# Twelve steps of seven tiles instead of fourteen of six, in a graph layer on one Trainium2 core

## The chip, the core and the metric

The kernel runs on one core of a Trainium2 chip. Its engines have queues of their own: PE multiplies matrices (PEld loads their weights), ACT and DVE work on whole tiles, POOL issues the gathers, and SP issues the direct loads and stores. The metric is the device time of one execution in microseconds; three runs of the kernel before were taken, and one further execution was profiled.

## The reference

The inputs are 6250 nodes with 64 features each, and 206250 edges that are sorted by their destination. The layer adds up, for each node, the normed features of its neighbours and the features of its edges, and puts the sum through two dense layers:

```python
h = jnp.maximum(_layernorm(x, axis=-1), 0.0)
msg = h[src] + edge_attr_64
agg = jax.ops.segment_sum(msg, dst, num_segments=6250)
x = x + (jax.nn.relu(agg @ W1 + b1) @ W2 + b2)
```

## The kernel before

**Neighbours by counting.** The sum over neighbours is a product of a matrix of counts (how often node `s` is a source for destination `d`) with `h`. The counts are made tile by tile. A tile holds up to 127 edges of three neighbouring destinations; 84 tiles are a block of 252 destinations, and 23 blocks make up the whole. For a tile DVE makes a row of one-hot digits (`encode`, L943 and L949, then `rows_of_tiles`, L960, into `hotb`), PE multiplies them (`count`, L973, one weight load and one product of 49 columns per tile, into `pc`, which has two buffers), and ACT copies the counts from `pc` into `ring` (L983). 49 products per block (`products`, L996) then multiply `ring` with `h`, each for 128 sources and all 252 columns of the block, into `pv`; a row of `ring` is one of these 49. The products of block b run while the counts of block b+1 are made.

**Steps.** The program is written step by step, and each engine takes its instructions in the order in which the steps were written. A step stands for `ST` = 6 tiles, a block has 14 steps, and each odd step counts a pair of steps, 12 tiles, and copies them in one instruction of 128 x 1764 elements. The last pair of a block is copied in two pieces: first the rows 0 to 12 of the 49 (432 elements), which the first run of products needs, then the other 37 (1332 elements). `PART` divides the 49 products in runs of 12, 12, 12 and 13, at the steps 1, 3, 5 and 7 of the next block. `ring` has a block's 252 columns and 144 fresh ones (`FRESH` = 8 steps), into which odd blocks write their first steps.

**Edge features.** Each block has six chunks of edges. SP loads them (`feat`), DVE makes their one-hot matrix (`hotf`, L505), PE sums them by node (`chunk_sum`, L518, into `bank`) at the steps 9, 11 and 11 of a block, and `chunk_place` (L550) adds the sums to `pv` at step 3. The last 17 groups of edges go another way: POOL gathers neighbour rows onto them (L361), PE sums them (L581), ACT copies (L583), DVE adds (L563).

**The order of the rest** is a set of tables by step number: which step turns the digits of 128 tiles (`TURNS`), clears `sums` (`CLEARS`), splits `h` into an upper and a lower part by thirds (`UPPERS`, ACT, L635; `LOWERS`, DVE, L639), or runs the second layer of a finished block (`LAYERS`; L1074, L1076, L1082, L1088).

**The head.** Before the steps come the layer norm and the first searches for where each tile's edges begin (`seek`, L384, on ACT). Five late searches stand behind the steps 5 to 9, and `place` (L389, L391, DVE) takes them up at step 10. Then a chain of small steps finds the tiles (up to fourteen) whose destinations have more than 127 edges: `second_ends` (L829, L830 on DVE; `pnext`, L832 on PE), `second_flags` (L839), `second_ranks` (L845, L847), `second_picks` (L861), `second_words` (L869). The first edge chunks wait for their destinations: a gather (`dstq`), `chunk_nodes` (L456, L457, DVE, step 5), and `chunk_turn` at step 6 (`pdst`, L464 on PE, and the copy into `rel`, L465 on ACT), which `hotf` reads.

## Time and profile before

| | us |
|---|---|
| median of three runs | 396.44 |
| lowest and highest of the three | 394.69, 398.32 |
| the profiled execution | 398.41 |
| span of the profile, first to last instruction | 396.7 |

The profiled execution lies 1.97 us above the median of the runs. The granted TensorE clock is 0.998 of full speed. In a list by engines the busy times overlap, since the engines work side by side; a busy share says nothing of who waits. The chain of waits is a path backwards from the last instruction; its shares add up to the span.

### The profile page before, as it was taken

Reading aid. Unit: us, or ns where it says so; the run is one execution under the profiler, and the core shown is the slowest. Engines: PE = TensorE matmul, PEld = TensorE weight load, DVE = VectorE, ACT = ScalarE, POOL = GpSimd, SP = SyncE. Lnnn points to the kernel's source line nnn. Section 1 sums busy time; section 2 is a strip of 40 time slices with the busy share of each in tenths; the row PEclk is TensorE's granted clock in tenths of the full one; section 3 lists DMA queues with packets and bytes.
Section 4 is the critical chain, followed back from the end, with each engine's and each line's share of the span. In section 5 each row is a group of like instructions: output and inputs, shape, how many; then the busy total and the mean of one; then the engine's idle time right before and its main releaser. Section 6 shows DMA issues by size and latency. Waiting matters only on the chain.

```text
span 396.7 us, 17221 instructions
## 1 busy us (share of the span) xinstructions
PE 339.1 (85%) x7303; PEld 308.0 (78%) x7304; DVE 307.0 (77%) x804; ACT 326.7 (82%) x380; POOL 268.0 (68%) x204
## 2 busy tenths in 40 slices
PE   2063589889989999999999799999999999999993
PEld 1052278779878879988899799989889889988983
DVE  5989477989986877968887788968886978696641
ACT  7586858798989779988799899988899889987750
POOL 7737768857857786668867578676866776766500
PEclk9999999999999999999999999999999999999999
DMA  8969765969865958869769669867958967887600
GB/s 170 266 202 327 238 172 99 256 158 226 216 181 130 266 131 215 238 142 267 190 167 258 180 158 266 235 160 206 257 127 220 269 176 181 212 215 176 165 10 25
DMA packets 111947, 76.89 MB, mean 194 GB/s; under 512 B 30855, under 2 KB 107775, under 8 KB 111865
## 3 DMA queue, kind: packets, MB, share of 16 engines
q1 hardware_dynamic: 91134, 67.20, 56.9%
q0 software_dynamic: 20560, 8.28, 15.9%
q8 instruction: 59, 0.97, 1.0%
q10 hardware_dynamic: 171, 0.26, 0.2%
q14 instruction: 23, 0.19, 0.2%
HBM read 71.45 MB, written 4.26 MB: 191 GB/s over the span
## 4 chain that ended last, share of the span: by engine, by line
PE 71%; ACT 12%; issue 7%; DVE 5%; DMA 3%; POOL 0%; DVEq 0%; ACTq 0%; SPq 0%; POOLq 0%
PE pv L996 30%; PE bank L518 14%; PE pc L973 12%; ACT ring L983 8%; PE ph L1074 3%; PE pv L550 2%; PE po L1082 2%; PE bank L581 2%; DMA dstq<-in_dst_g,cols_i 2%; PE pk L772 2%; DMA xl<-in_x 1%; ACT kq L792 1%; DVE sums L602 1%; ACT over L908 1%; PE pdst L464 1%
## 5 line engine op out<-in xcount | busy, mean ns | idle before, releaser
L983 ACT ACTIVATE ring<-pc 128x1764 fp32r<-128x1764 uint8 (+3 forms) x184 | 262.1, 1476 | 31.8 <-PE pc L973 19.3
L361 POOL DMA_INDIRECT pfeat<-table,src_p x132 | 222.3, 1684 | 80.0 <-PE bank L518 47.7
L996 PE MATMUL pv<-ring,h 128*128 128x252 f32 x1127 | 155.7, 287 | 10.6 <-ACT ring L983 6.0
L996 PEld LDWEIGHTS pv<-ring,h 128*128 128x128 f32 x1127 | 138.2, 190 | 13.2 <-ACT ring L983 7.2
L960 DVE TENSOR_TENSOR hotb<-at,of 127x576 int32<-127x576 bf16 x216 | 120.2, 599 | 2.1 <-PE pc L973 0.8
L973 PE MATMUL pc<-hotb 128*128 128x49 fp8e5 x1932 | 77.8, 186 | 4.4 <-ACT ring L983 2.3
L973 PEld LDWEIGHTS <-hotb 128*128 128x128 fp8e5 x1932 | 67.9, 98 | 14.1 <-issue 3.8
L518 PE MATMUL bank<-feat,hotf 128*18 128x64 f32 x3288 | 67.2, 224 | 7.7 <-issue 7.0
L518 PEld LDWEIGHTS bank<-feat,hotf 128*18 128x18 f32 x3288 | 52.6, 99 | 16.0 <-issue 13.3
L505 DVE TENSOR_TENSOR hotf<-rel,iota 128x432 f32<-128x432 bf16 x69 | 41.5, 601 | 6.3 <-PE ph L1074 3.0
L1031 DVE TENSOR_TENSOR sums<-sums,pv 128x252 f32<-128x252 f32 (+2 forms) x27 | 8.1, 328 | 23.8 <-PE pv L996 20.6
L943 DVE TENSOR_TENSOR at<-iota_a,kq 128x576 bf16<-128x576 bf16 (+1 forms) x54 | 24.2, 449 | 0.4
L307 PE MATMUL psrc<-shift,src 128*64 128x128 f32 (+1 forms) x16 | 4.1, 433 | 18.8 <-ACT src L304 18.8
L361 POOL DMA_INDIRECT words<-packed,first_i x15 | 16.4, 1091 | 5.6 <-issue 4.3
L361 POOL DMA_INDIRECT sums<-in_dst_g,row_i x15 | 16.2, 1079 | 4.8 <-issue 4.0
L949 DVE TENSOR_TENSOR of<-of,kv 128x288 bf16<-128x288 bf16 (+1 forms) x54 | 16.6, 308 | 2.6 <-ACT kv L800 0.2
L792 ACT ACTIVATE kq<-pk 128x512 bf16<-128x512 f32 (+18 forms) x48 | 17.9, 456 | 0.3 <-PE pc L973 0.3
L307 PEld LDWEIGHTS psrc<-shift,src 128*64 128x64 f32 (+1 forms) x16 | 3.1, 243 | 18.8 <-ACT src L304 14.1
L1074 PE MATMUL ph<-sums,w1s 128*128 128x252 f32 (+2 forms) x48 | 16.1, 416 | 1.9 <-ACT over L908 1.6
L943 DVE TENSOR_TENSOR of<-iota_w,kq 128x288 bf16<-128x288 bf16 (+1 forms) x54 | 16.2, 301 | 0.9 <-ACT kq L792 0.9
L1076 ACT ACTIVATE after<-ph,b1s 128x252 f32<-128x252 f32 (+2 forms) x24 | 11.5, 480 | 4.7 <-PE ph L1074 3.3
L1082 PE MATMUL po<-w2s,after 128*126 128x64 f32 (+2 forms) x96 | 15.1, 280 | 0.0
(190 smaller groups left out, 301.6 us busy)
## 6 DMA issues: line engine op xcount, KB each, us to landing
feat<-in_edge SPq DMA_DIRECT2D x137, 384.0 KB
pfeat<-in_edge SPq DMA_DIRECT2D x16, 256.0 KB
pfeat<-table,src_p POOLq DMA_INDIRECT x132
xl<-in_x SPq DMA_DIRECT2D x3, 512.0 KB
out_y<-after SPq DMA_DIRECT2D x22, 63.0 KB
table<-xl SPq DMA_DIRECT2D x2, 512.0 KB
after<-in_x SPq DMA_DIRECT2D x4, 252.0 KB
table<-xl SPq DMA_DIRECT2D x1, 544.0 KB
```

What stands on the lines that cost most here:

```text
L361: ins = nc.gpsimd.indirect_dma_start(out=rows, out_offset=None, in_=source, in_offset=bass.IndirectOffsetOnAxis(ap=index, axis=0), compute ...
L505: nc.vector.tensor_tensor(hot_of[u][:, :n].rearrange("p c j w -> p (c j) w"), rel[:, c:c + n].rearrange("p c q k -> p (c q k)").unsqueeze( ...
L518: ins = nc.tensor.matmul(bank[q * QP:q * QP + WQ, at:at + D], hot_of[u][:, c, j, :], feats[u][c][:, j, :], start=(k == 0), stop=(k == JP - 1))
L792: nc.scalar.activation(kq[:, q, at:at + n].rearrange("s i k o -> s (i k) o"), pk[:, q, a:a + n].rearrange("s i k -> s (i k)").unsqueeze(2) ...
L943: nc.vector.tensor_tensor(to[:, :n].rearrange("s i k (m o) -> s (i k) m o", o=2), iota_k.rearrange("s (m o) -> s m o", o=2).unsqueeze(1).t ...
L949: nc.vector.tensor_tensor(pairs_of, pairs_of, kv[:, c:c + n].rearrange("s i k o -> s (i k) o").unsqueeze(2) .to_broadcast([P, 2 * n, WE // ...
L960: nc.vector.tensor_tensor(hot[:SLOTS, :n, c:c + m * A8].rearrange("s i (w a) -> s i w a", a=A8), at[:SLOTS, o:o + n, k].unsqueeze(2).to_br ...
L973: nc.tensor.matmul(pc[:, j * WPC:j * WPC + HI], hot[:, :P], hot[:, P:P + HI], start=True, stop=True)
L983: done.append(nc.scalar.activation(to[:, h:z, :mid - u], of[:, h:z, u:mid, :V], AF.Copy))
L996: nc.tensor.matmul(pvs[b], h2[:, h, :], ring[:, h, c:c + columns_of_block(b)], start=(h == 0), stop=(h == HI - 1))
L1074: nc.tensor.matmul(ph[:, :n], w1s, agg[:, start[b]:start[b + 1]], start=True, stop=True)
L1082: nc.tensor.matmul(po[:pairs[b], k, :], hid[:, k:2 * pairs[b]:2], w2s, start=True, stop=True)
```

## The change

A step stands for seven tiles instead of six, and a block has twelve steps instead of fourteen. A pair is 14 tiles, so that a block has six counts and six copies (the last still in two pieces) instead of seven. The block's products run in three runs of 16, 16 and 17, at the steps 1, 3 and 5, and the first piece of the last copy holds 16 of the 49 rows. `ring` has 126 fresh columns (`FRESH` = 6 steps of 21 columns). `encode` takes 42 tiles at once instead of 36, `rows_of_tiles` 21 instead of 18. All tables by step number are scaled to the new steps, some by a step more or less. In the head the first `chunk_turn` moves from step 6 to step 5, ahead of the first late search.

```diff
-ST = 6
+ST = 7
-FRESH = 8
+FRESH = 6
-LOWERS = (11, 15, 17)
+LOWERS = (10, 13, 15)
-FIRST = 12
-PART = (0, 0, 12, 12, 24, 24, 36, 36, HI)
+FIRST = 16
+PART = (0, 0, 16, 16, 32, 32, HI)
-CHUNKS = ((9, 9), (11, 11), (11, 11))
+CHUNKS = ((7, 7), (9, 9), (9, 9))
-FIRST_CHUNKS = ((9, 9), (11, 11), (15, 15))
+FIRST_CHUNKS = ((8, 8), (10, 10), (13, 13))
...
-LAYERS = {10: 3, 5: 2}
+LAYERS = {8: 3, 4: 2}
...
-EB = 36
-HT = 18
-R = 7 * EB
+EB = 42
+HT = 21
+R = 6 * EB
...
     before = {
         2: [lambda: [fetch_h(g) for g in range(GA, GA + ROWS)]],
-        5: [lambda: chunk_nodes(0)],
-        6: [lambda: chunk_turn(0)],
+        4: [lambda: chunk_nodes(0)],
+        5: [lambda: chunk_turn(0)],
         10: [lambda: place(7, 8)],
```

How the order moves is shown at three places. In each row stands the line, the operation, what is written and what is read, and the size; numbers behind a name tell buffers apart, and the waits are by engine or DMA queue.

The first place is ACT in the head, from the third copy of counts (before) to the last late search:

```order
L983 ACTIVATE ring_402<-pc_486 128x49x36 [waits PE_49]
L384 ACTIVATE sums_72,first_215<-sums_72,nhalf_207 128x256 [waits DMASW5_49,Activation_49]
L635 ACTIVATE h2_73<-xl_93 128x16x64
L465 ACTIVATE rel_217<-pdst_503 128x384 [waits PE_49]
L384 ACTIVATE sums_72,first_215<-sums_72,nhalf_207 128x256 [waits DMASW6_49,Activation_49]
L983 ACTIVATE ring_402<-pc_512 128x49x36 [waits PE_49]
L384 ACTIVATE sums_72,first_215<-sums_72,nhalf_207 128x256 [waits DMASW7_49,Activation_49]
L635 ACTIVATE h2_73<-xl_93 128x16x64 [waits DVE_49]
L384 ACTIVATE sums_72,first_215<-sums_72,nhalf_207 128x256 [waits DMASW0_49,Activation_49]
L983 ACTIVATE ring_402<-pc_538 128x49x36 [waits PE_49]
L384 ACTIVATE sums_72,first_215<-sums_72,nhalf_207 128x256 [waits DMASW1_49,Activation_49]
```

The same place in the changed kernel, from the first split of `h`, which stands behind the second copy:

```order
L635 ACTIVATE h2_73<-xl_93 128x16x64
L465 ACTIVATE rel_217<-pdst_491 128x384 [waits PE_49]
L983 ACTIVATE ring_402<-pc_496 128x49x42 [waits PE_49]
L384 ACTIVATE sums_72,first_215<-sums_72,nhalf_207 128x256 [waits DMASW5_49,Activation_49]
L635 ACTIVATE h2_73<-xl_93 128x16x64 [waits DVE_49]
L384 ACTIVATE sums_72,first_215<-sums_72,nhalf_207 128x256 [waits DMASW6_49,Activation_49]
L983 ACTIVATE ring_402<-pc_521 128x49x42 [waits PE_49]
L384 ACTIVATE sums_72,first_215<-sums_72,nhalf_207 128x256 [waits DMASW7_49,Activation_49]
L635 ACTIVATE h2_73<-xl_93 128x17x64 [waits DVE_49]
L384 ACTIVATE sums_72,first_215<-sums_72,nhalf_207 128x256 [waits DMASW0_49,Activation_49]
L983 ACTIVATE ring_402<-pc_582 128x49x42 [waits PE_49]
L384 ACTIVATE sums_72,first_215<-sums_72,nhalf_207 128x256 [waits DMASW1_49,Activation_49]
```

The copy into `rel` (L465) has moved ahead of the third copy and of the first late search; three copies of counts now stand between it and the last search, where two stood.

The second place is DVE in the head, at the `place` that takes up the late searches (128x8). Before:

```order
L389 SCALAR_TENSOR_TENSOR first_215<-first_215,middle_205 128x8 [waits Activation_49]
L391 TENSOR_TENSOR first_i_216<-first_215,limit_212 128x8 [waits DVE_49]
L829 MEMSET ends_593 128x1
L830 TENSOR_SCALAR ends_593<-first_215 128x15
L639 TENSOR_TENSOR h2_73<-xl_93,h2_73 128x16x64
L839 SCALAR_TENSOR_TENSOR flag_601<-pnext_596,ends_593 128x15 [waits DVE_49,PE_49]
```

In the changed kernel:

```order
L389 SCALAR_TENSOR_TENSOR first_215<-first_215,middle_205 128x8 [waits Activation_49]
L391 TENSOR_TENSOR first_i_216<-first_215,limit_212 128x8 [waits DVE_49]
L639 TENSOR_TENSOR h2_73<-xl_93,h2_73 128x16x64
L829 MEMSET ends_638 128x1
L830 TENSOR_SCALAR ends_638<-first_215 128x15
L839 SCALAR_TENSOR_TENSOR flag_644<-pnext_641,ends_638 128x15 [waits DVE_49,PE_49]
```

The lower part of the first third of `h` (L639) now stands between `place` and `ends`, which `pnext` on PE reads.

The third place is ACT in a late block (no digits are turned there), from the first piece of a block's last copy to the last whole copy of the next. Before:

```order
L983 ACTIVATE ring_402<-pc_7359 128x12x36 [waits PE_49,Activation_49]
L983 ACTIVATE ring_402<-pc_7359 128x37x36 [waits Activation_49]
L983 ACTIVATE ring_402<-pc_7382 128x49x36 [waits PE_49]
L983 ACTIVATE ring_402<-pc_7417 128x49x36 [waits PE_49]
L583 ACTIVATE after_280<-bank_199 128x42 [waits DVE_49,PE_49]
L983 ACTIVATE ring_402<-pc_7465 128x49x36 [waits PE_49]
L983 ACTIVATE ring_402<-pc_7496 128x49x36 [waits PE_49]
L983 ACTIVATE ring_402<-pc_7529 128x49x36 [waits PE_49,Activation_49]
L1076 ACTIVATE after_280<-ph_7581,b1s_257 128x252 [waits PE_49,Activation_49]
L983 ACTIVATE ring_402<-pc_7584 128x49x36 [waits PE_49,Activation_49]
```

In the changed kernel:

```order
L983 ACTIVATE ring_402<-pc_7242 128x16x42 [waits PE_49,Activation_49]
L983 ACTIVATE ring_402<-pc_7242 128x33x42 [waits Activation_49]
L983 ACTIVATE ring_402<-pc_7267 128x49x42 [waits PE_49]
L983 ACTIVATE ring_402<-pc_7308 128x49x42 [waits PE_49]
L583 ACTIVATE after_280<-bank_199 128x42 [waits DVE_49,PE_49]
L983 ACTIVATE ring_402<-pc_7362 128x49x42 [waits PE_49]
L983 ACTIVATE ring_402<-pc_7401 128x49x42 [waits PE_49,Activation_49]
L1076 ACTIVATE after_280<-ph_7458,b1s_257 128x252 [waits PE_49,Activation_49]
L983 ACTIVATE ring_402<-pc_7461 128x49x42 [waits PE_49,Activation_49]
```

One whole copy is gone, each of the others is a sixth longer, and the first piece has 16 rows of 42 instead of 12 rows of 36.

## Rows read from the trace of the kernel before

**Rows 1.** Page, parts 1 and 4: busy time; chain by engine and line
```profile
PE 339.1 (85%) x7303; PEld 308.0 (78%) x7304; DVE 307.0 (77%) x804; ACT 326.7 (82%) x380; POOL 268.0 (68%) x204
...
PE 71%; ACT 12%; issue 7%; DVE 5%; DMA 3%; POOL 0%; DVEq 0%; ACTq 0%; SPq 0%; POOLq 0%
PE pv L996 30%; PE bank L518 14%; PE pc L973 12%; ACT ring L983 8%; PE ph L1074 3%; PE pv L550 2%; PE po L1082 2%; PE bank L581 2%; DMA dstq<-in_dst_g,cols_i 2%; PE pk L772 2%; DMA xl<-in_x 1%; ACT kq L792 1%; DVE sums L602 1%; ACT over L908 1%; PE pdst L464 1%
```

**Rows 2.** Windows: stretch, length, busy (x) of PE, PEld, DVE, ACT, POOL
```profile
0.00:56.58 56.58, 23.10 (x311) 17.55 (x312) 40.40 (x108) 38.48 (x69) 38.15 (x63) 1.00 0.85 239
56.58:253.69 197.11, 184.34 (x4108) 169.05 (x4109) 164.60 (x435) 174.02 (x196) 144.09 (x90) 1.00 0.76 194
253.69:367.20 113.51, 108.16 (x2491) 99.90 (x2491) 90.06 (x223) 100.67 (x102) 80.87 (x51) 1.00 0.79 205
367.20:396.70 29.50, 23.46 (x396) 21.46 (x396) 11.96 (x41) 13.52 (x16) 4.93 (x3) 0.98 0.25 65
```

**Rows 3.** Groups by shape, ACT copies: busy us, mean ns, idle before
```profile
L983 ACT ACTIVATE ring<-pc 128x1764 fp32r<-128x1764 uint8 x137 | 223.6, 1673 | 11.0 <-PE pc L973 7.5 <-PE pv L996 1.2 <-PE pnext L833 1.2
...
L983 ACT ACTIVATE ring<-pc 128x1332 fp32r<-128x1332 uint8 x22 | 28.2, 1280 | 0.0
...
L983 ACT ACTIVATE ring<-pc 128x432 fp32r<-128x432 uint8 x22 | 11.7, 531 | 20.8 <-PE pc L973 11.8 <-PE pk L772 9.0
```

**Rows 4.** Timeline of PE, block 15: start us, us, instruction [idle before]
```profile
266.08 0.47 PE L973 MATMUL pc<-hotb 128*128 128x49 fp8e5 x12
...
266.88 0.46 PE L973 MATMUL pc<-hotb 128*128 128x49 fp8e5 x12
268.16 1.67 PE L996 MATMUL pv<-ring,h 128*128 128x252 f32 x12 [0.82 <-ACT ring L983]
269.68 0.47 PE L973 MATMUL pc<-hotb 128*128 128x49 fp8e5 x12
269.99 1.64 PE L996 MATMUL pv<-ring,h 128*128 128x252 f32 x12
271.56 0.55 PE L550 MATMUL pv<-select,after 128*64 128x42 f32 x12
272.04 0.47 PE L973 MATMUL pc<-hotb 128*128 128x49 fp8e5 x12
...
274.83 1.74 PE L996 MATMUL pv<-ring,h 128*128 128x252 f32 x13
276.42 0.47 PE L973 MATMUL pc<-hotb 128*128 128x49 fp8e5 x12
```

**Rows 5.** Timeline of ACT at the same block start
```profile
267.58 4.77 ACT L983 ACTIVATE ring<-pc 128x432 fp32r<-128x432 uint8 x4 [0.76 <-PE pc L973]
```

**Rows 6.** Chain of waits in the head: first destinations land
```profile
30.57 7.16 DMA dstq<-in_dst_g,cols_i
```

**Rows 7.** Timeline of PE at the end of the head
```profile
42.23 1.15 PE L518 MATMUL bank<-feat,hotf 128*18 128x64 f32 x26 [1.35 <-issue]
...
49.50 0.58 PE L832 MATMUL pnext<-ends,shift 128*128 128x15 f32 x2
...
50.94 1.48 PE L518 MATMUL bank<-feat,hotf 128*18 128x64 f32 x48
...
56.58 2.93 PE L996 MATMUL pv<-ring,h 128*128 128x252 f32 x12
```

**Rows 8.** Timeline of ACT there: fifth copy, last search
```profile
46.73 1.64 ACT L983 ACTIVATE ring<-pc 128x1764 fp32r<-128x1764 uint8 x1 [0.48 <-remote]
48.27 0.50 ACT L384 ACTIVATE sums<-sums,nhalf 128x256 bf16<-128x256 int32 x1
...
48.76 1.10 ACT L635 ACTIVATE h<-xl 128x1088 fp32r<-128x1088 f32 x1
```

**Rows 9.** Timeline of DVE there: place, and the lower third
```profile
48.89 0.17 DVE L389 SCALAR_TENSOR_TENSOR first<-first,middle 128x8 f32<-128x8 f32 x1 [4.00 <-ACT ring L983]
...
49.26 1.22 DVE L639 TENSOR_TENSOR h<-xl,h 128x1024 fp32r<-128x1024 f32 x1
```

More of the change, by code (lines that the diff above doesn't have):

```diff
@@ L1019, in gnn_kernel @@
     spare["hotp"] = [a.rearrange("p (j w) -> p j w", j=J) for a in hots_p]
-    SECONDS = [(SB + 1) * STEPS + FRESH + 1 + 4 * k for k in range(-(-NX // 2))]
+    SECONDS = [(SB + 1) * STEPS + FRESH + 1 + 3 * k for k in range(-(-NX // 2))]
     def add_products(b):
@@ L1203, in gnn_kernel @@
     for n in range(2 * RP):
[L1204 removed]
+        before.setdefault(92 + 12 * n, []).append(lambda n=n: inside_rel(n))
     behind = {n: [lambda i=n + 5: seek(i, 1)] for n in range(5, 10)}
@@ L1237, in gnn_kernel @@
         c0, c1 = columns(i)[0][2], columns(i)[-1][2] + columns(i)[-1][1] - columns(i)[-1][0]
-        n = min((n for n in range(deadline(c0) + 1 - TURN[-1][0]) if n % STEPS in (TURNS if i > 2 else (6,)) and c1 - R <= encoded(n)),
+        n = min((n for n in range(deadline(c0) + 1 - TURN[-1][0]) if n % STEPS in (TURNS if i > 2 else (4,)) and c1 - R <= encoded(n)),
                 key=lambda n: (i > 2 and TURNS.index(n % STEPS), -n))
@@ L1241, in gnn_kernel @@
             steps = [n - k for k in (UNPACK if i > 2 else (4, 3, 2, 1))]
-            before.setdefault(max(steps[0] - 16, 3), []).append(lambda i=i: i > 2 and queue.insert(
+            before.setdefault(max(steps[0] - 14, 3), []).append(lambda i=i: i > 2 and queue.insert(
                 0, (WORDS_US * 2, lambda: fetch_pair(i))))
@@ L1251, in gnn_kernel @@
     for t in range(1, NT):
-        n = 78 + 14 * t
+        n = 66 + 12 * t
         before.setdefault(n, []).append(lambda t=t: t > 1 and queue.insert(0, (GATHER_US, lambda: fetch_dst(t))))
-        n = 49 if t == 1 else 86 + 14 * t
+        n = 42 if t == 1 else 73 + 12 * t
         before.setdefault(n, []).append(lambda t=t: chunk_nodes(t))
-        before.setdefault(n + (3 if t == 1 else 2), []).append(lambda t=t: chunk_turn(t))
+        before.setdefault(n + 2, []).append(lambda t=t: chunk_turn(t))
     def clock(n):
@@ L1262, in gnn_kernel @@
     for g in range(len(kept)):
-        n = 40 + 4 * g if g < 2 else 94 if kept[g][2] == 2 else XB * g * STEPS + 10
+        n = 34 + 4 * g if g < 2 else 80 if kept[g][2] == 2 else XB * g * STEPS + 8
         before.setdefault(n, []).append(lambda g=g: residual(g))
-        before.setdefault(min(n + (12 if g < 2 else 16), NSTEP - 1), []).append(lambda g=g: add_b2(g))
+        before.setdefault(min(n + (10 if g < 2 else 14), NSTEP - 1), []).append(lambda g=g: add_b2(g))
     ready = []
```

43 lines of the change are left out of this document (21 added, 22 removed).

## Prediction

> **What bounds the kernel now.** I read the busy times first, then the chain of waits, then the span cut into stretches, and last single block starts. PE is busy 85% of the span, ACT 82%, DVE 77%, and of the chain that ended last PE has 71%, ACT 12%, DVE 5% [rows 1]. So by the shares three engines are close to full, but the path runs through PE. The stretches say where [rows 2]: a head of 56.58 us up to the first products, thirteen blocks in 197.11 us (15.2 each), eight in 113.51 us (14.2 each) and a tail of 29.50 us. In the eight late blocks PE is busy 108.16 of 113.51 us, in the thirteen 184.34 of 197.11; ACT is busy 174.02 there. PE's work is thus nearly the length of a block, and what is left is little more than one wait in each block. That wait is seen at a block's start [rows 4]: PE issues the last count of the block before at 266.08, a product of the second layer, the next block's first count at 266.88, and then nothing until 268.16, when the first run of products starts. It waits 0.82 us for ACT. ACT in turn starts the first piece of the last copy at 267.58 after 0.76 us without work [rows 5]. So at a block's start neither engine is full; a short chain (last count, first piece, first run) sets the pace, and the length of the first piece lies on it.
>
> **PE's own work** hardly changes: the same number of counts and of products, sums and second layers. What changes lies in how it is cut.
>
> (a) The first piece grows from 12 rows of 36 to 16 rows of 42 columns, 432 to 672 elements. The pieces cost 531 ns at 432 and 1280 ns at 1332 elements [rows 3], 0.832 ns an element; 240 more are 0.20 us. PE waits for it at 22 starts, which is +4.4 us if nothing covers it. Ends: 0 (the first count and whatever else PE does there covers it) and 4.4. I take 4.4, since PE and ACT were both idle right there [rows 4, 5].
>
> (b) A pair's first count lies inside this wait and costs PE nothing; it now has 14 tiles, so the counts outside it have 70 tiles of a block instead of 72. A count of 12 takes 0.31 us from its start to the next start (269.68 to 269.99) [rows 4], 0.026 us a tile: -0.05 us a block, -1.1 us in 22. Nothing suggests a fixed cost per count, but the trace can't exclude it; with one of 0.1 us it would be -2.2 more.
>
> (c) One run of products less. A run of 12 takes 1.52 or 1.57 us, the one of 13 takes 1.59 (274.83 to 276.42) [rows 4]; at the pace of the latter 12 would be 1.47. So a run costs 0.05 to 0.10 us in itself, or nothing if what follows it makes the difference. I take 0.05: -1.1 us; ends 0 and -2.2.
>
> (d) In odd blocks the columns wrap at 126, a multiple of a chunk's 42, instead of 144, so no chunk is placed in two parts: one product less (two rows of the trace) in eleven blocks. Twelve such rows take 0.48 us (271.56 to 272.04) [rows 4], so 0.08 us a block, -0.9 us.
>
> **(e) ACT and DVE.** ACT's copies of a block now cost 6 x 1.673 + 1.280 + 0.531 = 11.85 us [rows 3]. A whole copy of 14 tiles is, by the same slope, 1.673 + 294 x 0.00083 = 1.92 us, and the two pieces are 0.73 and 1.32: 5 x 1.92 + 2.05 = 11.65, 0.20 us less. It counts only where ACT's copies are on the path. They have 8% of the chain, 31.7 us [rows 1]; 22 first pieces of 0.531 are 11.7 of it, whole copies the other 20. A saving of 0.20 in 11.85 on those is -0.3 us. Ends: 0, and -4.2 us, if ACT bounded all 21 middle blocks. DVE issues 56 operations fewer, but it has 5% of the chain, most of it ahead of the steps; I take nothing, with an end of -0.5 us. The longer look ahead of DVE, and POOL's and SP's queues, whose order stays but for single neighbours, I cost at nothing: PE's idle time is at the block starts, and the row there names ACT.
>
> **(f) The head.** The turn of the first chunk can't come earlier than its destinations, which land 7.16 us after 30.57 [rows 6]. It now stands ahead of the first late search and of a split on ACT, so `rel`, and with it the first sums on PE (42.23) [rows 7], can come earlier by up to a split and a search, 1.6 us [rows 8]; DVE's work ahead of it, one-hot tiles that are a sixth larger, takes part of that back, and I take 0.5 us. But more is now queued behind it. Before, the last search starts at 48.27, behind the fifth copy (46.73) [rows 8]; `place` follows at 48.89 [rows 9], and `pnext` at 49.50 [rows 7]. In the changed order ACT has, from `rel` to the last search, one whole copy more (1.92 us), two copies 0.25 us longer each, one search more (0.5) and the split of the last third, which stood behind the last search and takes 1.10 us [rows 8]: 4.0 us, less the 0.5 us that `rel` comes earlier. Then DVE does the lower part of the first third, 1.22 us [rows 9], between `place` and `ends`; before it came behind them. That makes `pnext` 3.5 + 1.2 = 4.7 us later, at 54.2. PE takes its instructions in order, so the count, the ranks, the picks and the first products wait behind it. Part comes back: the sums of the second chunk (50.94, 1.4 us) [rows 7] now stand ahead of `pnext`, and 28 tiles instead of 36 are counted behind it (0.2 us). First products: 56.58 + 4.7 - 1.6 = 59.7, +3.1 us. The first run there took 2.93 us [rows 7] instead of 1.52; it was held up by nothing that the trace names, and a PE that has idled before may be held up less. I take +2.0; ends -1.0 (the earlier `rel` wins and the rest is hidden) and +3.5.
>
> **The sum.** (a) +4.4, (b) -1.1, (c) -1.1, (d) -0.9, (e) -0.3, (f) +2.0: +3.0 us. Against the profiled execution of 398.41 us that is 401.4; the median of the runs is 1.97 us below it, and from 396.44 the forecast is 399.4 us. A measurement of this kernel can tell about 1%, 4 us, from no change, so this counts as no change.
>
> **A rule that speaks both ways.** In the rows of the block start ACT has idle time and PE waits for it. The Trainium skill (Perfetto Trace Analysis, Optimizing Scalar/DVE Operations) says that larger operations raise the throughput of an engine that is full, while one that isn't full and causes gaps on others should have its instructions broken up, so that work is completed sooner. By its first half the sum would be that of the first rival, by its second that of the second; the 0.76 us of idle ACT speak for the second half here.
>
> **Rivals.** *ACT is the bound after all.* In the thirteen early blocks it is busy 88% [rows 2], and they are 1 us longer than the late ones. If the copies bound the blocks, the first piece isn't seen, 21 blocks gain 0.20 us each, and (b) to (d) stay: -4.2 - 3.1 + 2.0 = -5.3, 391.1 us. Against it: the whole copies have only 20 us of the chain. It decides if ACT has no idle time ahead of the first pieces.
>
> *The first piece is paid at every block start, and nothing comes back.* That ends on the slower side: if a run's and a count's time is all pace and no fixed cost, and two tiles more of the first count are not hidden, (a) stands alone in the blocks: 4.4 - 0.3 + 2.0 = +6.1, 402.5 us. For it: the wait of 0.82 us at 268.16, and counts without a visible fixed cost. It decides when the first run starts 0.2 us later behind the last count while the rest of the block keeps its length.
>
> *The head keeps its length.* If the sums of the first chunk, which start earlier, rather than the searches end last, (f) is -1.0, and the sum is 0.0: 396.4 us. For it: the first sums take from 42.23 to 49.50, far more than such a run takes later. Against it: `pnext` followed `place` within a microsecond, so the searches ended together with the sums.
>
> **How the numbers follow.** The forecast has 0.40, ACT as the bound 0.17, the unpaid first piece 0.25, the unchanged head 0.18. A quarter of the forecast's own spread lies above 400.4, 1% over the median. Slower by over 1%: 0.25 x 0.9 + 0.40 x 0.25, 0.32; faster by over 1%: 0.17; the rest, 0.51, within. With (a) at 0 or 4.4, (c) and (e) at their ends and the head from -1.0 to +3.5 the range is 390.5 to 403.5: it takes in the first two rivals, and leaves out a fixed cost of a count together with a gain in the head, and a second wait that I don't see.
>
> **What would show it.** The first piece should take some 0.73 us, the wait of PE before the first run should be 0.2 us longer, and the late blocks should keep 14.2 us within 0.2. In the head, `pnext` should come at about 54 and the first products at 58 to 60. Whole copies should take 1.92 us. I am wrong if the early blocks fall below 14.9 us each (ACT was their bound), if the first products come before 57, or if a late block changes by more than 0.3 us.

## The result, and the profile after

The changed kernel takes 430.68 us (median of 6 runs, 428.20 to 433.49) against 398.20 us of the kernel before on the same chip: a ratio of 1.084, 95% interval 1.077 to 1.090. The forecast was 399.4 us with a range up to 403.5; it is wrong by some 31 us, and the range misses the time. The profiled execution takes 428.91 us (that of before 398.41); its span is 427.2 us, 30.5 us more than before.

The page of the changed kernel, its busy times, the granted clock in 40 slices, the chain by line and two groups:

```profile
PE 346.8 (81%) x7281; PEld 316.0 (74%) x7282; DVE 302.8 (71%) x748; ACT 329.7 (77%) x357; POOL 270.7 (63%) x204
...
PEclk9999999999999898988899899998999999999998
...
PE pv L996 32%; PE pc L973 12%; PE bank L518 11%; ACT ring L983 9%; PE ph L1074 3%; PE pv L550 3%; PE po L1082 2%; PE bank L581 2%; ACT over L908 1%; PE pk L772 1%; DVE hotb L960 1%; DVE xl L629 1%; DVE sums L613 1%; ACT kq L792 1%; ACT sums L384 1%
...
L983 ACT ACTIVATE ring<-pc 128x2058 fp32r<-128x2058 uint8 (+3 forms) x161 | 261.0, 1655 | 48.8 <-PE pc L973 40.7
...
L1074 PE MATMUL ph<-sums,w1s 128*128 128x252 f32 (+2 forms) x48 | 17.3, 444 | 16.6 <-ACT over L908 15.2
```

No engine has become the bound: PE, ACT and DVE all have a smaller share than in [rows 1]. Two things are new. PE's clock is below full speed in several slices of the middle, and the 48 products of `ph` have 16.6 us of idle time ahead of them, 15.2 of it put down to L908, which is `inside_rel` on ACT.

The windows say where the time lies. The columns are those of [rows 2]; the cuts here are the first products of blocks 1, 6, 15 and 23, first in the changed kernel:

```profile
0.00:57.77 57.77, 22.98 (x312) 17.52 (x314) 40.98 (x104) 39.67 (x68) 39.59 (x62) 1.00 0.88 236
57.77:134.10 76.33, 68.93 (x1560) 62.53 (x1556) 63.94 (x169) 66.32 (x67) 58.52 (x35) 1.00 0.69 176
134.10:297.77 163.67, 138.16 (x2865) 128.07 (x2860) 109.21 (x263) 123.03 (x130) 98.16 (x64) 0.92 0.68 173
297.77:410.45 112.68, 106.33 (x2469) 98.44 (x2465) 85.86 (x208) 98.22 (x89) 74.45 (x45) 1.00 0.73 187
410.45:427.20 16.75, 10.40 (x93) 9.45 (x93) 2.83 (x10) 2.42 (x6) 0.00 (x0) 0.87 0.08 20
```

and the kernel before at the same cuts, the third to the fifth of them:

```profile
132.03:268.16 136.13, 128.99 (x2868) 118.92 (x2868) 110.64 (x283) 120.38 (x139) 99.97 (x63) 1.00 0.79 203
268.16:380.39 112.23, 107.72 (x2479) 99.54 (x2479) 88.60 (x229) 98.47 (x97) 75.20 (x45) 1.00 0.75 194
380.39:396.70 16.31, 10.35 (x93) 9.38 (x93) 2.66 (x10) 2.51 (x6) 0.00 (x0) 0.96 0.07 20
```

Blocks 6 to 14 have grown by 27.5 us (136.13 to 163.67), and their mean granted clock has fallen from 1.00 to 0.92. For the same work PE is busy 9.2 us longer (138.16 against 128.99) and idle 18.4 us longer (25.51 against 7.14, the rest of each length): a slower PE and a waiting PE both have a part in it. The head (57.77 against 56.58, [rows 2]) has 1.2 us more, blocks 15 to 22 have 0.5, the tail 0.4, blocks 1 to 5 the remaining 0.9. So nearly the whole loss stands in nine blocks, and the late blocks, which have the same cut of seven tiles, are as long as before.

The view of waits for PE in that stretch (us in total, times, longest):

```profile
PE ph L1074 <- ACT over L908: 15.2, 8, 2.1
PE pdst L464 <- ACT kv L800: 4.4, 2, 2.3
...
PE pstart L409 <- ACT kv L800: 2.3, 1, 2.3
```

These are 21.9 us in eleven stops. In the same blocks of the kernel before, the view has no wait for L800, and one line for L908:

```profile
PE ph L1074 <- ACT over L908: 1.6, 2, 1.3
```

The timelines show what the three have in common. First PE, from the head, blocks 8 and 9, and a late block start:

```profile
53.54 0.61 PE L832 MATMUL pnext<-ends,shift 128*128 128x15 f32 x2 [3.87 <-DVE ends L830]
...
57.77 3.67 PE L996 MATMUL pv<-ring,h 128*128 128x252 f32 x16
...
186.33 0.69 PE L1074 MATMUL ph<-sums,w1s 128*128 128x252 f32 x2 [1.80 <-ACT over L908]
...
187.30 2.66 PE L518 MATMUL bank<-feat,hotf 128*18 128x64 f32 x96
...
196.68 0.61 PE L464 MATMUL pdst<-shift,dstq 128*128 128x128 f32 x3 [2.29 <-ACT kv L800]
...
197.48 3.56 PE L996 MATMUL pv<-ring,h 128*128 128x252 f32 x16
...
202.39 2.23 PE L996 MATMUL pv<-ring,h 128*128 128x252 f32 x17
...
309.73 0.52 PE L973 MATMUL pc<-hotb 128*128 128x49 fp8e5 x14
...
312.13 2.14 PE L996 MATMUL pv<-ring,h 128*128 128x252 f32 x16 [0.80 <-ACT ring L983]
```

then ACT, ahead of the stops at 186.33 and 196.68:

```profile
183.77 1.90 ACT L983 ACTIVATE ring<-pc 128x2058 fp32r<-128x2058 uint8 x1 [0.41 <-PE pc L973]
185.56 0.59 ACT L908 ACTIVATE over<-rel,edge_w 128x411 f32<-128x411 bf16 x1
...
194.12 1.96 ACT L983 ACTIVATE ring<-pc 128x2058 fp32r<-128x2058 uint8 x1
195.90 0.73 ACT L800 ACTIVATE kv<-pw 128x392 bf16<-128x392 f32 x2
197.33 0.49 ACT L465 ACTIVATE rel<-pdst 128x384 bf16<-128x384 f32 x1 [0.70 <-PE pdst L464]
```

`over`, `ph`, `pw`, `pdst` and `pstart` all ask for the PSUM tag "po", which has one buffer. `over` is written by ACT behind a whole copy of 1.90 us, and `ph`, PE's next instruction, can have the buffer only after that. `pw` is read by L800 behind another whole copy, and `pdst` waits for it.

The step numbers say why this is new, and for two of the stops the places of the digit turns do. `inside_rel` stands at step 92 + 12n, that is step 8 of blocks 7 to 14, and `mlp_hidden` is now issued at step 8 as well (LAYERS); before, 106 + 14n was also step 8, but `mlp_hidden` came at step 10, with counts and sums between. In block 8 `chunk_turn` stands at step 3, one behind the `value_powers` (L800) of step 2, where it stood two behind (4 and 2); before, a count and a run of products lay between `pw` and `pdst`, and `pdst` did not wait:

```profile
167.24 0.65 ACT L800 ACTIVATE kv<-pw 128x512 bf16<-128x512 f32 x1
```

```profile
168.00 0.61 PE L464 MATMUL pdst<-shift,dstq 128*128 128x128 f32 x3
```

In blocks 6 and 9 the kernel before turned no digits (among the blocks 6 to 10 its `pw` stands in 7, 8 and 10). In the changed kernel the turns fall into 6, 8 and 9, so that the `pstart` of block 6, at step 3 in both kernels, and the `pdst` of block 9 have got a `value_powers` ahead of them.

The second loss follows the first. The window of the run of products behind the stop at 196.68:

```profile
197.40:201.40 4.00, 4.00 (x38) 3.78 (x34) 1.33 (x3) 2.31 (x2) 3.39 (x3) 0.57 0.21 21
```

PE is busy all the time, at a mean granted clock of 0.57, and the 16 products take 3.56 us, where 17 take 2.23 at 202.39. Cut into half microseconds, the trace has eight such stretches in blocks 6 to 14, at the lower level (1.2 GHz) for about 3.5 us each; seven begin within 1.5 us behind one of the eleven stops, one in the last microsecond of one.

### The profile page after: what moved, and what is told of

Read it like the earlier page. It is cut to its first block, busy times and chain, and to the rows that moved or that the text cites. A ratio compares the mean times of both kernels' runs of the same rounds, so it can differ in the third digit from the quotient of the medians.

```text
span 427.2 us, 17112 instructions
## 1 busy us (share of the span) xinstructions
PE 346.8 (81%) x7281; PEld 316.0 (74%) x7282; DVE 302.8 (71%) x748; ACT 329.7 (77%) x357; POOL 270.7 (63%) x204
## 4 chain that ended last, share of the span: by engine, by line
PE 69%; ACT 12%; issue 7%; DVE 6%; DVEq 0%; ACTq 0%
PE pv L996 32%; PE pc L973 12%; PE bank L518 11%; ACT ring L983 9%; PE ph L1074 3%; PE pv L550 3%; PE po L1082 2%; PE bank L581 2%; ACT over L908 1%; PE pk L772 1%; DVE hotb L960 1%; DVE xl L629 1%; DVE sums L613 1%; ACT kq L792 1%; ACT sums L384 1%
## 5 line engine op out<-in xcount | busy, mean ns | idle before, releaser
L983 ACT ACTIVATE ring<-pc 128x2058 fp32r<-128x2058 uint8 (+3 forms) x161 | 261.0, 1655 | 48.8 <-PE pc L973 40.7
L996 PE MATMUL pv<-ring,h 128*128 128x252 f32 x1127 | 154.7, 291 | 9.8 <-ACT ring L983 5.4
L996 PEld LDWEIGHTS pv<-ring,h 128*128 128x128 f32 x1127 | 141.0, 194 | 11.9 <-ACT ring L983 6.3
L960 DVE TENSOR_TENSOR hotb<-at,of 127x672 int32<-127x672 bf16 (+1 forms) x184 | 116.4, 677 | 3.1 <-PE pc L973 2.5
L518 PE MATMUL bank<-feat,hotf 128*18 128x64 f32 x3288 | 70.5, 235 | 6.4 <-issue 6.0
L518 PEld LDWEIGHTS bank<-feat,hotf 128*18 128x18 f32 x3288 | 56.7, 106 | 13.6 <-issue 10.5
L1031 DVE TENSOR_TENSOR sums<-sums,pv 128x126 f32<-128x126 f32 (+1 forms) x27 | 8.1, 328 | 53.3 <-PE pv L996 39.2
L1074 PE MATMUL ph<-sums,w1s 128*128 128x252 f32 (+2 forms) x48 | 17.3, 444 | 16.6 <-ACT over L908 15.2
L943 DVE TENSOR_TENSOR at<-iota_a,kq 128x672 bf16<-128x672 bf16 x46 | 23.1, 502 | 0.0
L528 DVE COPY after<-bank 128x384 f32<-128x384 f32 (+1 forms) x23 | 12.7, 551 | 14.4 <-PE pc L973 9.0
L1076 ACT ACTIVATE after<-ph,b1s 128x252 f32<-128x252 f32 (+2 forms) x24 | 11.2, 467 | 15.1 <-PE ph L1074 14.0
L1074 PEld LDWEIGHTS ph<-sums,w1s 128*128 128x128 f32 x48 | 7.4, 195 | 19.3 <-ACT over L908 16.6
L361 POOL DMA_INDIRECT sums<-in_dst_g,row_i x15 | 17.3, 1155 | 4.8 <-issue 4.3
L949 DVE TENSOR_TENSOR of<-of,kv 128x336 bf16<-128x336 bf16 x46 | 15.4, 335 | 2.0 <-issue 0.2
```

The costliest lines, as they stand in the source:

```text
L361: ins = nc.gpsimd.indirect_dma_start(out=rows, out_offset=None, in_=source, in_offset=bass.IndirectOffsetOnAxis(ap=index, axis=0), compute ...
L518: ins = nc.tensor.matmul(bank[q * QP:q * QP + WQ, at:at + D], hot_of[u][:, c, j, :], feats[u][c][:, j, :], start=(k == 0), stop=(k == JP - 1))
L943: nc.vector.tensor_tensor(to[:, :n].rearrange("s i k (m o) -> s (i k) m o", o=2), iota_k.rearrange("s (m o) -> s m o", o=2).unsqueeze(1).t ...
L949: nc.vector.tensor_tensor(pairs_of, pairs_of, kv[:, c:c + n].rearrange("s i k o -> s (i k) o").unsqueeze(2) .to_broadcast([P, 2 * n, WE // ...
L960: nc.vector.tensor_tensor(hot[:SLOTS, :n, c:c + m * A8].rearrange("s i (w a) -> s i w a", a=A8), at[:SLOTS, o:o + n, k].unsqueeze(2).to_br ...
L983: done.append(nc.scalar.activation(to[:, h:z, :mid - u], of[:, h:z, u:mid, :V], AF.Copy))
```

## Experiments

The theory: the loss comes from the new order of the steps, in which tables were scaled each for itself, so that ACT's use of the one buffer "po" now stands directly ahead of PE's next use; PE's queue stops, and its clock falls behind some of the stops. Rival 1: the coarser cut itself (longer copies, later counts) costs the time. Rival 2: the clock falls by itself, and the waits are small beside it. The runs fell on chips that ran the kernel before in 376 to 396 us, so results are compared by their ratio to the kernel before on the same chip.

**One pair apart: `inside_rel`.**

```
-        before.setdefault(92 + 12 * n, []).append(lambda n=n: inside_rel(n))
+        before.setdefault(93 + 12 * n, []).append(lambda n=n: inside_rel(n))
```

> The changed kernel with one number altered: inside_rel's eight passes stand at step 9 of blocks 7 to 14, one step behind mlp_hidden instead of in the same step ahead of it. Theory (TensorE's queue is stopped by the one-buffer tile that both use): the 15.2 us of waits of ph for L908 go to under 2 us, blocks 7, 8 and 9 keep what pdst costs, the granted clock of blocks 11 to 14 returns to 0.98 or more and each of these is 14.0 to 14.8 us long instead of 16.1 to 17.8; the whole 408 to 414 us. Rival 1 (the coarser cut itself costs the time: longer copies, later counts): blocks 11 to 14 stay over 16 us and the whole over 425. Rival 2 (the clock falls by itself, the waits are small beside it): the waits go, the clock stays under 0.93 there, the whole 414 to 420.

Measured: 395.53 us against 378.05, ratio 1.048 (1.043 to 1.054). The waits for L908 are gone, blocks 11 to 14 are 14.0, 15.0, 13.3 and 14.1 us long at a clock of 1.00. Blocks 8 and 9 stay at 19.1 and 18.8 us with a clock of 0.91: their stops are those of `pdst`, 2.1 and 2.3 us, and the clock still falls behind both:

```profile
PE pdst L464 <- ACT kv L800: 4.4, 2, 2.3
```

One number takes back somewhat less than half of the loss. On the scale of 398 us it is 417, over the expected 408 to 414 and within the 414 to 420 of rival 2; but that rival wanted the clock of blocks 11 to 14 under 0.93, and it is full.

**The other pair apart: `chunk_turn` and `chunk_starts`.**

```
-        75: [lambda: chunk_starts(2 * RC, NC)],
+        81: [lambda: chunk_starts(2 * RC, NC)],
...
-        n = 42 if t == 1 else 73 + 12 * t
+        n = (42, 97, 121, 157)[t - 1]
...
-        before.setdefault(n + 2, []).append(lambda t=t: chunk_turn(t))
+        before.setdefault(n + (8 if t == 2 else 2), []).append(lambda t=t: chunk_turn(t))
```

(`chunk_rows` and `chunk_quarters` follow `chunk_starts` at 82 and 83.)

> The changed kernel with the other pair taken apart: chunk_turn of the third piece stands at step 9 of block 8, of the fourth and fifth at step 3 of blocks 10 and 13 (which have no value_powers ahead), and chunk_starts of the later chunks with its two followers at steps 9 to 11 of block 6. inside_rel stays where the change put it. Theory: the 4.4 us of pdst behind L800 and the 2.3 us of pstart are gone, block 6 returns to 15.0 to 15.5 us, block 9 loses 2 to 4 us, blocks 11 to 14 stay at 16 to 18 us; the whole 419 to 424 us. Rival 1 (the coarser cut itself): within 2 us of the changed kernel, 428 to 433. Rival 2 (the clock falls by itself): only the 6.7 us of waits come back at most, and blocks 6 and 9 keep a clock under 0.93.

Measured: 404.27 us against 378.05, ratio 1.069 (1.062 to 1.076). PE no longer waits for L800, but `ph` still waits for L908, and the clock of blocks 6 to 14 stays at 0.93:

```profile
PE ph L1074 <- ACT over L908: 14.7, 8, 1.9
```

Against the changed kernel (1.084 and 1.089, the second below) the gain is 1.5 to 2 points, 6 to 8 us, about what the waits for L800 were. It ends 1 or 2 us above what was expected on the scale of 398 us (426), as `pstart` and `pdst` have got new, shorter waits, 0.9 and 0.6 us, behind L1076 at step 8.

**Both pairs apart (the mended kernel).** The edits of the run before, and `inside_rel` where TensorE's next use of the buffer is four steps off:

```
-        before.setdefault(92 + 12 * n, []).append(lambda n=n: inside_rel(n))
+        before.setdefault(124 + 12 * n, []).append(lambda n=n: inside_rel(n))
```

> Both pairs taken apart in the changed kernel: turns and starts as in the run before this, inside_rel at step 4 of blocks 10 to 17, where TensorE's next use of the tile is four steps away. Theory: waits of TensorE for L908 and L800 under 2 us in all, granted clock 0.98 or more in blocks 6 to 14, blocks 10 to 14 of 14.0 to 14.6 us; what is left is the forecast's own sum and some single waits of blocks 2 and 19: 398 to 405 us. Rival 1 (the coarser cut itself): over 415. Rival 2 (the clock falls by itself): 406 to 414 with the clock under 0.95 in some of the blocks 6 to 14.

Measured: 383.59 us against 378.05, ratio 1.017 (1.011 to 1.022), that is 405 us on the scale of 398: the theory's upper end. Windows of the mended kernel, blocks 6 to 14 together and block 11:

```profile
129.50:257.69 128.19, 124.58 (x2859) 116.60 (x2859) 107.87 (x262) 118.23 (x124) 99.47 (x63) 1.00 0.83 216
...
202.72:216.01 13.29, 13.29 (x324) 12.60 (x321) 10.26 (x24) 13.29 (x15) 10.61 (x8) 1.00 0.87 228
```

PE is busy in all of block 11, and the clock is full. The cut of seven tiles, the longer copies and the later counts are all still in this kernel, so rival 1 falls: at most the 1.7% that are left could be its own.

**The mechanism in the kernel before.** Six tiles a step, and `inside_rel` put into the step of `mlp_hidden`:

```
-        before.setdefault(106 + 14 * n, []).append(lambda n=n: inside_rel(n))
+        before.setdefault(108 + 14 * n, []).append(lambda n=n: inside_rel(n))
```

> The kernel before with one number altered: inside_rel stands at step 10 of its blocks 7 to 14, the step in which mlp_hidden is issued there, instead of step 8. Six tiles a step and the fine counts are kept. Theory: ph waits for L908 in each of eight blocks, 1.5 to 2.1 us each, and the granted clock of these blocks falls under 0.95; the whole 12 to 20 us over the kernel before, 410 to 418. Rival 1 (the coarser cut itself, and the waits only go with it): within 4 us of the kernel before. Rival 2 (the clock falls by itself in the changed kernel): 8 blocks lose the wait alone and keep a clock of 0.98 or more, 408 to 413.

Measured: 387.14 us against 378.05, ratio 1.025 (1.020 to 1.031), 9.1 us. The view of waits for PE:

```profile
PE ph L1074 <- ACT over L908: 12.7, 8, 1.6
```

and the window of blocks 6 to 14:

```profile
124.22:261.94 137.72, 124.98 (x2870) 117.15 (x2869) 110.63 (x283) 122.37 (x139) 98.71 (x63) 1.00 0.78 202
```

One moved call makes the kernel before slower by 9 us, through the same wait. The theory was only half right: it wanted 12 to 20 us and a falling clock, and the clock stays at 1.00 behind all eight stops, which is what rival 2 had put down (the wait alone, 408 to 413 us; on the scale of 398 us it is 408). So this run shows the price of the wait, and leaves rival 2 standing. The stops are 1.55 to 1.61 us long here, those of the changed kernel 1.80 to 2.3 us.

**The changed kernel on a second chip.** No edit.

> The changed kernel itself, unaltered, beside the others on one chip, so that their sums can be made against one trace. The chip of the runs on step numbers ran the kernel before in 378.05 us instead of 398.20. Theory: the same stops give the same microseconds, 27 to 33 us over the kernel before, a ratio of 1.07 to 1.09, and the granted clock falls in the same blocks 6 to 9, 11, 13 and 14. Rival 1 (the coarser cut itself costs the time) gives no other number here. Rival 2 (the clock falls by itself): the falls stand in other blocks than the waits.

Measured: 410.54 us against 376.27, ratio 1.089 (1.082 to 1.096). The same three waits have 14.7, 4.1 and 1.7 us. The windows of blocks 6 to 14 and of block 11:

```profile
129.57:287.52 157.95, 137.03 (x2858) 127.41 (x2859) 108.95 (x262) 122.99 (x130) 97.93 (x64) 0.91 0.70 179
...
222.91:239.66 16.75, 14.89 (x325) 14.04 (x321) 10.40 (x23) 13.80 (x15) 10.46 (x8) 0.90 0.71 182
```

Among the blocks 6 to 14 the clock falls in 6, 8 to 12 and 14 (on the first chip in 6 to 9, 11, 13 and 14), each time behind a stop or at its end, so the blocks are not those expected, and the 34.3 us over the kernel before are a little more than the expected 27 to 33. Which stops are followed by a fall differs from run to run; that it stands at a stop does not.

**The stops filled with work.** Products of ones, which nobody reads, ahead of the eight `ph` and of two `pdst`; ahead of `pstart`, which the expectation names as well, the run had none:

```
+    def fill(k):
+        of = ps.tile([P, 512], F32, tag="pv", name="fill")[:, :P]
+        for _ in range(k):
+            nc.tensor.matmul(of, onesb, onesb, start=True, stop=True)
...
         made[b >= NW] = start[b + 1]
+        if marks:
+            marks.clear()
+            fill(30)
...
+        if t in (2, 3):
+            fill(36)
         pt = ps.tile([P, JP, P], F32, tag="po", name="pdst", bufs=1)
```

(`inside_rel` sets the mark, so only the `ph` behind it gets the products.)

> The changed kernel with idle TensorE made busy: 30 products of a 128 x 128 tile of ones into a spare buffer stand ahead of each of the eight ph that wait for L908, 36 ahead of two pdst and of pstart; their results are read by nobody. The waits stay, TensorE works through them. Theory (a wait costs its own length, and a second time because the clock is halved for some microseconds behind it): the granted clock is 0.98 or more in blocks 6 to 14, and the time falls by 6 to 12 us against the changed kernel on the same chip. Rival 1: the clock has no part in the loss, the time stays within 3 us. Rival 2 (the clock falls by itself): it falls in the same blocks in spite of the filling.

Measured: 401.47 us against 376.27, ratio 1.066 (1.060 to 1.072), 9.1 us less than the changed kernel on this chip. The windows of blocks 6 to 14 and of block 11:

```profile
128.98:277.21 148.23, 145.07 (x3170) 135.40 (x3171) 109.49 (x262) 122.99 (x130) 96.85 (x63) 0.99 0.73 189
...
216.70:231.93 15.23, 15.15 (x355) 14.28 (x350) 10.00 (x22) 13.47 (x15) 9.91 (x7) 1.00 0.72 193
```

With 312 more products the kernel is faster. The only fall left in these blocks begins at 135.5 us, behind `pstart`, the stop that was not filled. So the falls come from PE's idle time, which ends rival 2, and filling seven of the eight takes back 9 us. What is left against the mended kernel (148.23 and 128.19 us in these blocks, on two chips of nearly the same speed) is 20.0 us: the waits themselves, the one fall, and what the filling costs. The windows of the changed kernel on this chip and of the mended one give the same division without filling. PE is busy 137.03 us in the one and 124.58 in the other, 12.4 us more or 1.6 for each of the eight falls, and idle 20.92 and 3.61 us, 17.3 us more.

**The first piece as before.** In the mended kernel:

```
-FIRST = 16
-PART = (0, 0, 16, 16, 32, 32, HI)
+FIRST = 12
+PART = (0, 0, 12, 12, 30, 30, HI)
```

> The mended kernel with the first piece of each block's last copy cut back from 16 to 12 numbers of a node's 49, and the runs of products at 12, 18 and 19 instead of 16, 16 and 17. It measures the prediction's first term by itself. Theory (that term was sized rightly): the first product of 22 blocks comes 0.18 us earlier, 4.0 us less than the mended kernel, 379 to 380 on the chip that ran that in 383.59, ratio 1.005 to 1.010. Rival: the start of a block is not bound by the first piece, and the time stays within 1.5 us of the mended kernel.

Measured: 383.36 us against 376.27, ratio 1.018 (1.012 to 1.023), no gain on the mended kernel's 1.017 that the two intervals could show, where 4.0 us (1.1 points) were expected. The first pieces are shorter and the time is not. By the second half of the rule weighed in the prediction (the Trainium skill, Perfetto Trace Analysis, Optimizing Scalar/DVE Operations) breaking up such pieces may let work be completed sooner. No run here shows a gain from that.

**The opening set back.** In the mended kernel:

```
-LOWERS = (10, 13, 15)
+LOWERS = (11, 13, 15)
...
-    behind = {n: [lambda i=n + 5: seek(i, 1)] for n in range(5, 10)}
+    behind = {n: [lambda i=n + 6: seek(i, 1)] for n in range(4, 9)}
```

> The mended kernel with two pieces of the opening moved back: the five late searches (L384 with their flips) start at step 4 instead of 5, so that the last stands ahead of the whole copy of step 9 on ScalarE, and the first lower third of h (L639, 1.22 us) stands behind ends on VectorE. Theory (the head's term was sized rightly, and the searches are its cause): ends comes 2.5 to 3.1 us earlier than in the mended kernel, the first products 2.0 to 2.8 us earlier, at 54.2 to 55.0 instead of 56.98, and the whole is 2 to 3 us shorter. Rival: pnext comes earlier and the first products wait for the last copy of the block instead, less than 1 us is gained.

Measured: 379.84 us against 376.27, ratio 1.011 (1.006 to 1.017). The timeline of DVE,

```profile
48.91 0.17 DVE L389 SCALAR_TENSOR_TENSOR first<-first,middle 128x8 f32<-128x8 f32 x1 [4.32 <-ACT sums L384]
...
49.21 0.17 DVE L830 TENSOR_SCALAR ends<-first 128x15 f32<-128x15 f32 x1
...
49.29 1.22 DVE L639 TENSOR_TENSOR h<-xl,h 128x1024 fp32r<-128x1024 f32 x1
```

and of PE:

```profile
49.43 0.61 PE L832 MATMUL pnext<-ends,shift 128*128 128x15 f32 x2 [3.08 <-DVE ends L830]
...
53.66 1.20 PE L996 MATMUL pv<-ring,h 128*128 128x252 f32 x4
```

In the mended kernel DVE has, at the same place:

```profile
51.10 0.17 DVE L389 SCALAR_TENSOR_TENSOR first<-first,middle 128x8 f32<-128x8 f32 x1 [6.58 <-ACT sums L384]
...
52.53 0.17 DVE L830 TENSOR_SCALAR ends<-first 128x15 f32<-128x15 f32 x1
```

`place` comes 2.2 us earlier, `ends` follows it after 0.30 instead of 1.43 us, and the first products come at 53.66 instead of 56.98; the last two are a little earlier than expected. On the same chip the kernel with the cut-back first piece took 383.36 us, 3.5 more. The searches and the lower third are what the opening waited for.

**The kernel before, for a trace.** No edit.

> The kernel before, unaltered, for a trace of it on the chip of the other experiments. Theory: blocks of 13 to 15 us, TensorE stops behind L908 and L800 under 2 us in all, the granted clock 1.00 in every block, first products at 54 to 55.5 us; 374 to 379 us. No rival gives another number; the trace shows how much of the mended kernel's 5 to 7 us stands in the blocks 1 to 5, which I expect to be 2 to 3.5 us.

Measured: 396.02 us against 396.26, ratio 0.999. The run fell on a slower chip than the others before it, so its trace could not be set beside the mended kernel's, and how much of the mended kernel's excess stands in blocks 1 to 5 stays open by this run. The run with `inside_rel` moved in the kernel before answers it: its blocks 1 to 5 are those of before, it ran on the mended kernel's chip, and the windows give 69.50 us there and 72.52 in the mended kernel, 3.0 us, as expected. Of these, 1.7 us are PE's busy time (66.43 and 68.12) at a clock of 0.95 instead of 1.00. The trace serves the next run.

**Three more places apart.** The opening set back, and:

```
-                add_later(n + 5)
+                add_later(n + 4)
...
-        81: [lambda: chunk_starts(2 * RC, NC)],
+        82: [lambda: chunk_starts(2 * RC, NC)],
...
-        before.setdefault(n + (8 if t == 2 else 2), []).append(lambda t=t: chunk_turn(t))
+        before.setdefault(n + (9 if t == 2 else 2), []).append(lambda t=t: chunk_turn(t))
```

> The mended kernel with the opening set back, and three more places where scaled or hand-set step numbers meet: add_sums comes one step earlier (step 7, where it was in the step of ph), pdst and pstart of the later pieces one step later than in the mended kernel (step 10 instead of 9, where they stood behind L1076). Theory: the two waits of ph for L563 (2.0 us) and those of pdst and pstart for L1076 (1.9 us) go, blocks 6, 8, 12 and 19 get about 1 us shorter each, the whole 3 to 4 us less than with the opening set back alone: 375.5 to 377, ratio to the kernel before 0.998 to 1.005. Rival (the coarser cut costs something of its own everywhere): the ratio stays at 1.008 or more.

Measured: 395.92 us (12 runs) against 396.26, ratio 0.997 (0.994 to 1.000). Windows of blocks 6 to 14, of this kernel

```profile
134.22:268.95 134.73, 128.23 (x2866) 118.40 (x2861) 106.87 (x262) 118.90 (x124) 98.41 (x63) 1.00 0.80 205
```

and of the kernel before on the same chip:

```profile
130.48:266.90 136.42, 129.07 (x2868) 118.96 (x2868) 111.01 (x285) 120.74 (x139) 101.41 (x64) 1.00 0.80 205
```

With the collisions gone and the opening set back the coarser cut is as fast as the fine one on this chip, with these blocks 1.7 us shorter. The profiled execution is one of the longer ones (398.86 us): its blocks 1 to 5 take 79.16 us against 74.35, with two falls of the clock. The loss of 8 to 9% was the order of the steps: some 7 points the two pairs, the rest the opening and the three places together.

**The first chunk's turn back at its step.** The opening set back, and `chunk_nodes(0)` and `chunk_turn(0)` at 5 and 6:

```
-        4: [lambda: chunk_nodes(0)],
-        5: [lambda: chunk_turn(0)],
+        5: [lambda: chunk_nodes(0)],
+        6: [lambda: chunk_turn(0)],
```

> The mended kernel with the opening set back, and with chunk_nodes and chunk_turn of the first piece at steps 5 and 6, as before the change, instead of 4 and 5: the second half of the change undone. Theory (that move is worth little, since the late searches set the end of the opening): first products within 1 us of 53.66, the whole within 2 us of 379.84. Rival (the move is what keeps the opening short): rel comes a step later, the sums of the first block behind it, and the whole is 2.5 us or more longer.

Measured: 399.17 us against 396.26, ratio 1.008 (1.004 to 1.011); with the opening set back alone it was 1.011 on another chip. The first products come at 54.61 us; on this chip the kernel with three more places apart, whose opening differs mainly in that step, has them at 55.06. The earlier turn is worth nothing that these runs can tell.

**The third `hotf` a step earlier.** The kernel with three more places apart, and:

```
-HOT_AT = (3, 5, 8)
+HOT_AT = (3, 5, 7)
```

> The same as the run with three more places taken apart, and the third hotf of each block one step earlier (step 7 instead of 8), so that VectorE has it ready before the sums of step 9. Theory (step numbers that meet are what is left): the three waits of the sums for L505 in blocks 1, 2 and 4 (2.5 us) go, 1 to 2.5 us less than without it: 373.5 to 376. Rival: VectorE's queue is only ordered anew and ph or the counts wait in place of the sums, no gain.

Measured: 406.33 us against 396.26, ratio 1.025 (1.020 to 1.031), 2.9 points slower than without. The rival was right. The view of waits for PE in blocks 6 to 14:

```profile
PE ph L1074 <- DVE after L1088: 7.7, 4, 3.6
```

`mlp_add` (L1088) reads `po`, the same buffer, on DVE at step 7; now `hotf` is issued ahead of it in that step, the buffer comes free later, and `ph` of step 8 stops. One number again, and the same buffer.

## Why the prediction was wrong

**The step that failed** is one sentence of (e): "The longer look ahead of DVE, and POOL's and SP's queues, whose order stays but for single neighbours, I cost at nothing: PE's idle time is at the block starts, and the row there names ACT." The single neighbours were the cost. Every table of step numbers was scaled from fourteen steps to twelve and rounded by itself. `inside_rel` and `mlp_hidden` use one buffer from two engines; they were two steps apart and came to stand in one step. `value_powers` and `chunk_turn` came from two steps apart into neighbouring ones in block 8, and in blocks 6 and 9 a turn of digits came to stand ahead of `pstart` and `pdst` where there had been none. None of the terms (a) to (f) looks at such a pair. On the faster chips the waits cost 17 to 20 us (PE's idle time, and the filled against the mended kernel), the clock behind them 9 to 12 us (the changed against the filled kernel, and PE's busy time). The profile had a hint: L908 has 1% of the chain [rows 1], though it runs eight times for 0.6 us; PE already waited for it twice.

The prediction's range is also not what its terms give: with the ends that it names for (a), (c), (e) and (f) it would be 387.0 to 402.3 us instead of 390.5 to 403.5. The measured time lies far outside of both.

**(a) First piece.** It takes 734 ns instead of 531 [rows 3], as forecast, and whole copies take 1918 ns (forecast 1.92 us); the groups by shape of the changed kernel:

```profile
L983 ACT ACTIVATE ring<-pc 128x2058 fp32r<-128x2058 uint8 x114 | 216.7, 1918 | 24.8 <-PE pc L973 23.5 <-PE bank L518 0.7
...
L983 ACT ACTIVATE ring<-pc 128x672 fp32r<-128x672 uint8 x22 | 16.2, 734 | 24.0 <-PE pc L973 17.2 <-PE pk L772 4.6 <-PE bank L518 1.7
```

But the +4.4 us did not come. PE's wait at a late block start is 0.80 us (312.13, above) where it was 0.82 [rows 4], and in the whole trace the products wait 5.4 us for ACT's copies where they waited 6.0. So the term does not show on the first chip either, though a cut-back piece was not tried on it. Cutting the piece back in the mended kernel gained nothing, and in the mended kernel the products wait for ACT's copies 0.3 us in all.

**(b), (c), (d), and (e) for ACT**, small gains, can't be told apart in these runs. Together with (a) they were to add 0.4 us in the eight late blocks (1.0 us over 22); measured is 0.5, and a single wait of `ph` for `add_sums` (L563), one more pair in one step, is 1.4. Without it the blocks would be 0.9 us shorter than before. The kernel with all found pairs apart, at 0.997, has a reordered opening as well, so what the cut is worth by itself stays open.

**(f) The head.** `pnext` comes at 53.54 us (forecast 54.2), and it waits 3.87 us for `ends`, as the working said. The first products come at 57.77 us, 1.2 us later than before, where the sum took 2.0. The run with the opening set back shows the cause to be the forecast one: the late searches and the lower third.

**The rivals.** ACT did not become the bound: blocks with full PE remained, and its share fell. The kept head and the unpaid first piece would both have ended within 2% of the kernel before; nothing among the rivals could reach 430. The rival that was missing is a new wait between two engines in the middle blocks, though the prediction did name "a second wait that I don't see" as left out.

## What to carry to other kernels

When a table of step numbers is scaled, list for each shared buffer, above all one with a single copy, its users in order of step before and after, with the engine of each. Here a pair of users on two engines that came closer than one long instruction of the slower engine was a stop of the other's whole queue, at every repeat. Users that the program places by itself, as the turns of digits here, belong on the list too. A stop of TensorE may be paid twice, since its clock may be halved behind it. TensorE's busy and idle time in the windows of the two kernels tell the two prices apart, and so does one run with idle products in the stops. That a kernel with the same work and less overhead becomes slower by 8% speaks for such a collision, and one number moved by a step can prove it.

## What had not been expected of the hardware

**The clock falls behind short stops.** In the changed kernel TensorE's granted clock was at the lower level for about 3.5 us in eight places of blocks 6 to 14, after stops of 1.80 to 2.29 us, with TensorE busy before and behind them; three of the eleven stops were followed by no fall. Behind eight stops of 1.55 to 1.61 us in the kernel of six tiles there was none. The length of one stop does not decide it: of these two, the first (the cut-back first piece) was followed by a fall at 94.0 us, the second (the third `hotf` a step earlier) by none:

```profile
93.53 0.31 PE L581 MATMUL bank<-after,pfeat 128*64 128x42 f32 x2 [1.58 <-DMA pfeat<-table,src_p]
```

```profile
178.21 0.66 PE L1074 MATMUL ph<-sums,w1s 128*128 128x252 f32 x2 [1.58 <-DVE after L1088]
```

In the mended kernel the clock fell at 101.4 us with no longer stop ahead of it than 0.67 and 0.54 us, close together. What decides was not tried. In block 11 of the second chip the fall and the filling differ by 1.5 us (16.75 against 15.23). The Trainium skill (TensorE: Matmul & The Clock Gate, HAM oscillation — how this bites in real kernels) tells of DMA waits that bring the clock down each time, so that the next stage starts slow. The traces agree that waits do it; here, at 1.80 to 2.29 us, they are waits for ScalarE. The Trainium skill (the same page, Terms) sets the penalty at the time spent slow times the share of the clock that is missing. By this formula 3.5 us at half speed would be an estimated 1.75 us; the filled run shows 1.5, and its filling has a cost of its own, and the busy time against the mended kernel 1.6.

**A fall whose cost does not show.** In the trace of the mended kernel the clock is also halved from 46.5 to 60.5 us, in the head, where PE waits 6.6 us for `ends`. One of its four runs had a mean clock of 0.997 instead of 0.972 to 0.981, and took 384.13 us, no less than the others (382.82 to 384.86); of that run there is no trace. Of the two traces of the kernel before, the later one has such a fall from 47.0 to 60.5 us and its first products at 56.13 us, the earlier one a full clock there and its first products at 56.58.

**Chips 5% apart.** The same program, the kernel before, took 376 to 378 us on two chips and 396 to 398 in the other runs, at a mean granted clock of 0.98 to 1.00 on either. The page lines for the sums L518 have 58.0 us of busy time in the run of the kernel before with `inside_rel` moved (on a fast chip) and 65.0 us in the later run of the kernel before (on a slow one), though one sum has a mean of 224 ns in both; L996 has 0.4 us of idle time ahead of it there and 9.6 us here, 8.1 of them for ACT's copies. What lies under that was not followed; the ratio of the changed kernel, 1.084 and 1.089, is nearly the same on both.
